# A vision tower on one core: head values in four quarters of the array, and a third pair turned early

## The chip, the cores and the metric

The kernel runs on one NeuronCore of one Trainium2 chip. The metric is the device time of one execution in microseconds (us). A core has five engines that run side by side and wait for each other by semaphores: TensorE (PE in the profile; its weight loads are PEld), VectorE (DVE), ScalarE (ACT), GpSimd (POOL) and SyncE (SP), which here issues most of the DMA transfers. Matrix products are written to PSUM, which has 8 banks of 128 partitions by 512 float32 numbers; everything else lies in SBUF, 128 partitions wide. All data is float32.

## The reference, cut to what matters

The input holds 32 images of 3 x 256 x 256. A tokenizer makes 256 tokens of 256 features of each. Layer 0 is a gated attention and a feed-forward part on selected tokens; layer 1 is a phasor memory and an FFN that is a small attention network of its own, with 4 heads of 64 features and 4 experts. The two parts that the change touches:

```python
def _L0_attn_ref(x, g, W_uv, ...):
    xn = x / jnp.maximum(norm, EPS) * g                 # x is the layer-normed token
    uv = jax.nn.silu(jnp.einsum('bnd,de->bne', xn, W_uv) + b_uv)
    u, v, base = uv[..., :H], uv[..., H:2*H], uv[..., 2*H:]
    q = base * gamma[0] + beta[0]
    k = base * gamma[1] + beta[1]
    attn = jnp.square(jax.nn.relu(einsum('bns,bms->bnm', q, k) * S**-0.5))
    return jnp.einsum('bnh,hd->bnd', u * jnp.einsum('bnm,bmh->bnh', attn, v), W_o) + b_o

def _L1_ffn_ref(x, hl_w, hl_b, wq, wk, wv, gate_w, ...):
    sx = jnp.einsum('bsh,ndh->bnsd', x, hl_w) + hl_b    # 4 heads of 64
    v = jnp.einsum('bnsd,nod->bnso', sx, wv)            # the head values
    ...                                                 # 4 experts: scores, softmax, att @ v
    ...                                                 # gate over the experts, two small layers
```

## The kernel before

The 32 images stay in SBUF as `H[b]` through all layers (two chunks of 128 tokens by 256 features). The work goes in stages: tokenizer (0 to about 180 us), attention of layer 0 (to 690), its feed-forward part (to 915), the memory of layer 1 (to 1246), the FFN of layer 1 (to the end). Within each stage the order of every engine's instructions is the order in which the program emits them (the schedule is by hand), so an instruction that waits holds back all that are emitted after it on its engine. DMA transfers go through SP's queue in the same way.

**Tokenizer and layer-0 attention.** The tokenizer loop (L384) makes one image per step: 12 products into one PSUM bank, emptied by DVE, which also takes the statistics; the patches of an image are loaded by SP five images ahead. Layer 0's attention works on pairs of images. A pair is prepared by `norm_b` (L261: four DVE instructions that normalise into `cx` tiles), `bias_b` (L268: POOL adds the output bias to `H`), and then its activations must be turned, feature-major, into a tile `xT`. There are two ways for that. `turn_b` (L273) transposes on TensorE and copies out of PSUM by ACT and DVE. `blocks_b` (L277) and `turned_b` (L289) do it without TensorE: DVE transposes blocks of 32 x 32 into the tile `blocks` (one buffer), SP stores it by four DMAs to a DRAM tile `b_turned`, and four more DMAs load it back, turned, as `bxT` (two buffers, L293).

Pairs 0 and 1 are normalised inside the tokenizer loop, after images B-6 and B-4, and turned on TensorE: pair 0 before the last image, pair 1 at the start of the attention loop. That loop (L535) is a pipeline by pairs: step t computes scores (`scores_b`), gates and values of pair t-1 (named old), base and queries of pair t (new), the gated product and output of pair t-2 (older), and prepares pair t+1 (next_one). In step t=1 the pair prepared is pair 2, whose `norm_b` and `blocks_b` stand after the gates and whose `turned_b` stands after `bias_b`. `base_b` (L295) of pair 2, in step t=2, is the first to read its `bxT`, directly behind the scores of pair 1.

**FFN of layer 1.** Each image passes through some 97 pieces (`PIECES`). A table `ROUND`, written out by hand, says in which order the pieces of eight images at different depths follow each other in one round; a table `END` does it for the last six images. In a round, TensorE's pieces come in this order: `experts` 0, `scores` 1, 0, 2, `experts` 1, `head_values`, `first_layer`, `heads`, `scores` 5, 4, 3, `second_layer`, and eight `outputs`. All heads have 64 features, and two heads share one 128-row tile, so products of heads have 64 rows. `experts` (L1180), `scores` and `head_values` (L1193) use two row groups of the array, 64 rows each by 128 columns, and write to two banks. `outputs` and `second_layer` use two column halves, 128 rows by 64 columns each. `first_layer` (L1433) and `heads` use the whole array, 128 rows by 128 columns.

`head_values` multiplies `sx` (features of two heads by 128 tokens, the stationary operand) by `WV` (64 rows by 80 columns, the moving operand) for two chunks of tokens, two head pairs and two row groups: 8 products. Each float32 product is two pairs of instructions, a weight load (LDWEIGHTS) and a MATMUL. Both banks of `im.pv` are emptied by DVE in `head_values_out` (L1204). All products are recorded under the helper's line, L118, so in the profile they are told apart by the names of their operands: `WV,sx` are the head values, `sx,A` the experts before them, `fxT,w_fc` the first layer behind them.

Of the kernel before, what the change touches and what calls it, by code (L numbers as in the profile page):

```python
# [40 lines left out]
P = 128  # L41
B, N, D = 32, 256, 256
# [38 lines left out]
def vit_tower(tc, a, out):  # L81
# [35 lines left out]
    def mm(o, lhsT, rhs, first=True, last=True):  # L117
        nc.tensor.matmul(o, lhsT, rhs, start=first, stop=last)  # L118
# [142 lines left out]
    def norm_b(b0, s):  # L261
        s.xs = []
        for j in range(2):
            x = px.tile([P, NC, D], F32, name="cx", bufs=8)
            normed(x, b0 + j, st_b)
            s.xs.append(x)

    def bias_b(b0, s):  # L268
        for j in range(2):
            h = H[b0 + j]  # L270
            nc.gpsimd.tensor_tensor(h, h, over(row_b("b_o"), [P, NC, D], 1), ALU.add)

    def turn_b(b0, s, pool, name):  # L273
        s.xT = pool.tile([P, 2, 2 * N], F32, name=name)
        transposed(s.xT, s.xs, copy_split)

    def blocks_b(b0, s):  # L277
        s.d = pdram.tile([32, 16 * NC, 4, 32], F32, name="b_turned", bufs=2)
        y = px.tile([P, 4 * N], F32, name="blocks", bufs=1)
        y = y.rearrange("p (f c t) -> p f c t", f=8, t=32)  # L280
        for j, x in enumerate(s.xs):
            nc.vector.transpose(
                y[:, :, j * NC : (j + 1) * NC, :].rearrange("p f c t -> p c f t"),
                x.rearrange("p c (f t) -> p c f t", t=32),
            )
        for i in range(4):
            nc.sync.dma_start(s.d[:, :, i, :], y[32 * i : 32 * i + 32].rearrange("p f c t -> p (f c) t"))
# [18 lines left out]
    with (  # L306
        tc.tile_pool(name="a_w", bufs=1) as pw,
        tc.tile_pool(name="a_x", bufs=6) as pp,
    ):


        PARTS = (1, 1, 2, 2)
        x0, tokW = [], []
        for k, n in enumerate(PARTS):
            f = sum(PARTS[:k])
            x, w = pw.tile([P, n, N], F32, name=f"patch0_{k}"), pw.tile([P, n, D], F32, name=f"tokW{k}")
            nc.sync.dma_start(x, patches[:, f : f + n, 0:N])
            nc.scalar.dma_start(w, a["tokW"][:, f : f + n, :])
            x0 += [x[:, i, :] for i in range(n)]
            tokW += [w[:, i, :] for i in range(n)]  # L320
        p = bank()
        for _ in range(3):
            mm(p[:, 0:N], zero[:, 0:P], zero)
        n_k, xs_a = len(tokW), {}

        def load_patches(b):
            xs_a[b] = pp.tile([P, n_k, N], F32, name="patch")
            nc.sync.dma_start(xs_a[b], patches[:, :, b * N : (b + 1) * N])

        load_patches(1)  # L330
        load_patches(2)
        row_a = load_rows(pw, "rows_a", ROWS_A, N_ROWS_A, nc.sync)
        nc.sync.dma_start(cols, a["cols"])
        for b in range(3, 6):
            load_patches(b)

        def layer_0_weights():
            return (
                load(wpool_b, "wuv", nc.sync), load_rows(wpool_b, "rows_b", ROWS_B, N_ROWS_B, nc.sync),
                load(wpool_b, "wo", nc.sync), load_rows(wpool, "rows_c", ROWS_C, N_ROWS_C, nc.sync),  # L340
                load(wpool, "before", nc.sync), load(p0, "w1", nc.sync),
            )

        def unit_a(b):
            if b == 0:
                ps = [bank() for _ in range(NC)]
                for k in range(n_k):
                    for c in range(NC):
                        mm(ps[c][:, 0:D], x0[k][:, c * P : (c + 1) * P], tokW[k], k == 0, k == n_k - 1)
                for c in range(NC):  # L350
                    nc.vector.tensor_tensor(H[b][:, c, :], ps[c][:, 0:D], row_a("tok_b"), ALU.add)
            else:
                x, p = xs_a.pop(b), bank()
                for c in range(NC):
                    for k in range(n_k):
                        mm(p[:, c * D : (c + 1) * D], x[:, k, c * P : (c + 1) * P], tokW[k], k == 0, k == n_k - 1)
                nc.vector.tensor_tensor(
                    H[b], p.rearrange("p (c d) -> p c d", c=NC), over(row_a("tok_b"), [P, NC, D], 1), ALU.add
                )
                if b + 5 < B:  # L360
                    load_patches(b + 5)
            st, _, i = at(st_b, b)
            for c in range(NC):
                stats(st, i, c, H[b][:, c, :])

        def powers_b(b):
            st, rs, i = at(st_b, b)
            q = slice(i * NC, (i + 2) * NC)  # L370
            var = st.rearrange("p i c s -> p (i c) s")[:, q, 1]
            low = spool.tile([P, 2 * NC], F32, name="low")
            pow_rstd(low, var)
            nc.gpsimd.tensor_scalar(rs[:, q], var, 1e-36, 1.0, ALU.max, ALU.mult)
            nc.gpsimd.tensor_tensor(rs[:, q], rs[:, q], minus_half[:, 0 : 2 * NC], ALU.pow)
            return rs[:, q], low

        def factors_b(rs, low):
            nc.vector.scalar_tensor_tensor(rs, low, 1e5, rs, ALU.mult, ALU.min)
            nc.vector.tensor_scalar(rs, rs, col("attn_g"), None, ALU.mult)  # L380

        for b in range(B):  # L384
            if b == B - 1:
                half = [p0.tile([P, 4, D], F32, name="cs", bufs=2).rearrange("p j d -> p (j d)") for _ in range(2)]
                turn_b(0, pairs_b[0], p0, "xsel")
                base_b(0, pairs_b[0], half[0][:, 0 : 2 * N])
                queries_b(0, pairs_b[0], half[0][:, 2 * N :], half[1][:, 0 : 2 * N])
            unit_a(b)  # L390
            if b == 4:
                wuv, row_b, wo, row_c, before, w1 = layer_0_weights()
            if b % 2:
                powers = powers_b(b - 1)
            elif b:
                factors_b(*powers)
            if b in (B - 6, B - 4):
                u = (b - B + 6) // 2
                norm_b(2 * u, pairs_b[u])
                bias_b(2 * u, pairs_b[u])  # L400

    def norm_c(b):
# [35 lines left out]
    with (  # L438
# [96 lines left out]
        for t in range(B // 2 + 2):  # L535
            new, old, older, next_one = pair(t) if t else None, pair(t - 1), pair(t - 2), pair(t + 1)
            next_one = next_one if t else None
            if t == 1:
                turn_b(*new, p2, "bxT")
            if t >= 4:  # L540
                turned = turn_weights(2 * (t - 4))
            if old:
                scores_b(*old)
            if new:
                base_b(*new, p2.tile([P, 2 * N], F32, name="base"))
            if t >= 4:
                ranks(2 * (t - 4), turned)
                if t in (5, 7):
                    first_ranks(2 * t - 10, quads[t // 2 - 2], 0)
            if new:  # L550
                queries_b(*new, p2.tile([P, 2 * N], F32, name="bq"), p2.tile([P, 2 * N], F32, name="bk"))
            if old:
                gates_b(*old)
            if t == 1:
                factors_b(*powers)
            if next_one:
                norm_b(*next_one)
                blocks_b(*next_one)
            if old and t >= 3:
                norms_c(2 * (t - 3))  # L560
            if old:
                values_b(*old)
            if next_one:
                bias_b(*next_one)
            if old and t >= 3:
                residuals_c(2 * (t - 3))
            if next_one:
                turned_b(*next_one, p2, "bxT")
            if t == B // 2 - 1:
                blocks_c(0, quads[0], 0)  # L570
                moved_c(0, quads[0], 0)
            if older:
                gated_b(*older)
                if t == B // 2 + 1:
                    norms_c(2 * (t - 3))
                    residuals_c(2 * (t - 3))
                output_b(*older)
# [531 lines left out]
    with (  # L1109
# [83 lines left out]
        def head_values(b, im):  # L1193
            im.pv = [bank(), bank()]
            for c in range(NC):
                for hp in range(2):
                    o = (2 * c + hp) * VC
                    for s, p in zip(halves, im.pv):
                        mm(p[:, o : o + VC], im.sx[s, hp, c * P : (c + 1) * P], WV[s, hp, :])

        def head_values_out(b, im, h):
            im.v = whole(im, "ev", [P, NC, NH, VC], p2)
# [789 lines left out]
```

## Time and profile before

| | |
|---|---|
| median of 3 runs | 1856.04 us (1854.69 to 1856.21) |
| the profiled execution | 1860.63 us, of it 1858.9 from the first to the last instruction |
| mean granted TensorE clock | 0.989 |
| PE busy in 180 to 690 us (attention, layer 0) | 507.47 us of 510 |
| PE busy in 1246 to 1780 us (FFN, layer 1) | 530.51 us of 534; DVE 470.69, ACT 441.91 |
| last 79 us | PE 50.81, DVE 73.46 |
| head values, `WV,sx` | 512 loads of 188 ns, 512 products of 267 ns mean |

How to read such lines. A timeline row gives the start, the length, the engine, the source line, the operation, the tiles written and read (`out<-in`), for a product rows*columns of the array and then rows x columns of the moving operand, and the count of instructions merged; in brackets stands the idle time before it and what ended it. Matmul durations include the way through the array, so a train of products is better read from the distance of their starts. A row of a table by stretches gives the stretch, its length, the busy time and number of instructions of each engine, the granted clock, the share of the DMA engines and GB/s.

### The profile page before, as it was taken

Reading aid. Unit: us, or ns where it says so; the run is one execution under the profiler, and the core shown is the slowest. Engines: PE = TensorE matmul, PEld = TensorE weight load, DVE = VectorE, ACT = ScalarE, POOL = GpSimd, SP = SyncE. Lnnn points to the kernel's source line nnn. Section 1 sums busy time; section 2 is a strip of 40 time slices with the busy share of each in tenths; the row PEclk is TensorE's granted clock in tenths of the full one; section 3 lists DMA queues with packets and bytes.
Section 4 is the critical chain, followed back from the end, with each engine's and each line's share of the span. In section 5 each row is a group of like instructions: output and inputs, shape, how many; then the busy total and the mean of one; then the engine's idle time right before and its main releaser. Section 6 shows DMA issues by size and latency. Waiting matters only on the chain.

```text
span 1858.9 us, 36581 instructions
## 1 busy us (share of the span) xinstructions
PE 1814.4 (98%) x14284; PEld 1277.1 (69%) x14284; DVE 1345.4 (72%) x3595; ACT 810.0 (44%) x1640; POOL 614.0 (33%) x697
## 2 busy tenths in 40 slices
PE   9999999999999999999999999999999999999993
PEld 7887567676666677676654555557777778778772
DVE  2335477878888664543578778764899999999998
ACT  0001222222222211212244544547888888888883
POOL 1223133434343334333434333323222232222330
PEclk9999999999999999999999999999999999999996
DMA  8551212121212134333321221222344443434432
GB/s 291 165 153 35 46 42 61 52 63 44 59 41 63 37 109 145 108 100 99 96 80 68 91 78 70 80 63 58 101 107 103 106 106 104 108 99 110 101 99 67
DMA packets 193171, 167.50 MB, mean 90 GB/s; under 512 B 70880, under 2 KB 166112, under 8 KB 192608
## 3 DMA queue, kind: packets, MB, share of 16 engines
q1 hardware_dynamic: 186272, 147.51, 28.0%
q0 software_dynamic: 6144, 16.79, 3.1%
q8 instruction: 115, 1.88, 0.4%
q10 hardware_dynamic: 576, 0.79, 0.1%
q14 instruction: 64, 0.52, 0.1%
HBM read 82.98 MB, written 57.41 MB: 76 GB/s over the span
## 4 chain that ended last, share of the span: by engine, by line
PE 92%; DVE 5%; ACT 1%; DMA 1%; issue 1%; SPq 0%; DVEq 0%; ACTq 0%
PE bank L118 91%; DMA patch<-in_patches_dram 0%; PE bank L516 0%; DVE eo L1353 0%; DVE fout L1504 0%; DVE ranges L1376 0%; DVE six L126 0%; ACT dex L945 0%; DVE two L1361 0%; ACT et L1229 0%; ACT two L945 0%; DVE dz L991 0%; DVE dxB L199 0%; DVE dx L837 0%; DMA b_turned<-blocks 0%
## 5 line engine op out<-in xcount | busy, mean ns | idle before, releaser
L1238 POOL TENSOR_SCALAR_AFFINE_SELECT et<-et 128x512 f32<-128x512 f32 (+1 forms) x192 | 170.1, 895 | 395.8 <-ACT et L1229 291.5
L1229 ACT ACTIVATE et<-bank 128x512 f32<-128x512 f32 x384 | 202.7, 625 | 0.1
L118 PE MATMUL bank<-ev,et 128*64 128x72 f32 (+1 forms) x6144 | 194.0, 225 | 2.5 <-ACT et L1229 1.3
L118 PEld LDWEIGHTS bank<-ev,et 128*64 128x64 f32 x6144 | 190.0, 137 | 7.5 <-issue 3.8
L118 PE MATMUL bank<-g,sw 64*128 64x256 f32 (+1 forms) x512 | 178.7, 490 | 0.0
L118 PE MATMUL bank<-g,sx 64*128 64x256 f32 (+1 forms) x512 | 178.3, 489 | 0.0
L118 PE MATMUL bank<-tokW,patch 128*128 128x256 f32 x768 | 169.3, 384 | 2.1 <-DMA patch<-in_patches_dram 2.1
L118 PEld LDWEIGHTS bank<-tokW,patch 128*128 128x128 f32 x768 | 148.0, 193 | 23.7 <-issue 2.9
L118 PE MATMUL bank<-bxT,w_wuv 128*128 128x512 f32 x300 | 132.9, 598 | 2.5 <-DMA bxT<-b_turned 2.5
L118 PEld LDWEIGHTS bank<-g,sx 64*128 64x128 f32 x512 | 92.7, 187 | 52.3 <-issue 43.6
L864 ACT ACTIVATE hT<-bank,cols 128x512 f32<-128x512 f32 x64 | 44.0, 687 | 186.9 <-PE bank L118 186.9
L118 PE MATMUL bank<-wvo,dm 128*128 128x512 f32 x256 | 114.3, 599 | 0.0
L118 PE MATMUL bank<-w_wo,gT 128*128 128x256 f32 x512 | 113.2, 379 | 0.0
L118 PE MATMUL bank<-attn,bv 128*128 128x256 f32 x512 | 113.1, 379 | 0.0
L118 PE MATMUL bank<-w_w,hT 128*128 128x256 f32 x512 | 112.3, 380 | 0.0
L118 PE MATMUL bank<-xsel,w_w 128*128 128x512 f32 x256 | 111.4, 593 | 0.0
L118 PEld LDWEIGHTS bank<-attn,bv 128*128 128x128 f32 x512 | 97.3, 190 | 19.5 <-issue 7.2
L126 DVE BATCH_NORM_STATS2 six<-h 128x6 f32<-128x256 f32 x256 | 105.6, 413 | 4.4
L118 PEld LDWEIGHTS bank<-w_w,hT 128*128 128x128 f32 x512 | 97.1, 190 | 15.5 <-issue 2.9
L118 PEld LDWEIGHTS bank<-w_wo,gT 128*128 128x128 f32 x512 | 97.3, 190 | 13.3 <-DVE gT L489 0.2
L118 PE MATMUL bank<-w_wuv,bxT 128*128 128x512 f32 x240 | 105.5, 592 | 0.0
L118 PEld LDWEIGHTS bank<-bxT,w_wuv 128*128 128x128 f32 x300 | 57.6, 192 | 68.6 <-issue 67.8
(292 smaller groups left out, 3567.9 us busy)
## 6 DMA issues: line engine op xcount, KB each, us to landing
patch<-in_patches_dram SPq DMA_DIRECT2D x31, 768.0 KB, 4.6
exT<-normed SPq DMA_DIRECT2D x32, 256.0 KB, 3.6
sw<-sx SPq DMA_DIRECT2D x64, 128.0 KB, 2.4
er_turned<-eblk SPq DMA_DIRECT2D x31, 256.0 KB, 2.8
fraw<-er_turned SPq DMA_DIRECT2D x62, 128.0 KB, 3.3
both<-fxT SPq DMA_DIRECT2D x62, 128.0 KB, 2.3
both<-hx SPq DMA_DIRECT2D x62, 128.0 KB, 2.3
out_dram<-fout SPq DMA_DIRECT2D x31, 256.0 KB, 2.2
```

The lines of the kernel that those rows point to most:

```text
L118: nc.tensor.matmul(o, lhsT, rhs, start=first, stop=last)
L126: nc.vector.bn_stats(six, x)
L864: nc.scalar.activation(s.hT[:, m, :], p, AF.Gelu_apprx_tanh, bias=col("b1", m))
L1229: nc.scalar.activation(t2[:, i, :], p, AF.Exp)
L1238: nc.gpsimd.affine_select(out=own, in_=own, pattern=[[0, 2 * n_e], [1, P]], compare_op=ALU.is_ge, fill=0.0, base=0, channel_multiplier=-1,)
```

## The change

Two independent edits. In the attention of layer 0, three pairs instead of two are prepared in the tokenizer: after images B-8, B-6 and B-4 pairs 0, 1 and 2 are normalised and get their bias; for pair 2 the block transposes and the four stores to DRAM follow there too. The four loads of pair 2's `bxT` move to the top of step t=1, directly behind pair 1's `turn_b`, and step t=1 prepares no pair any more.

In the FFN of layer 1, each head-value product of 64 rows by 128 columns is made as two of 64 rows by 64 columns: the 128 tokens of a chunk are taken in two halves `q`, and the result of each half goes to the partitions `q` of the same bank. With two row groups, the four products of a step lie in the four quarters of the array. The moving operand, the sums and the banks stay as they are.

```diff
@@ tokenizer loop
-            if b in (B - 6, B - 4):
-                u = (b - B + 6) // 2
+            if b in (B - 8, B - 6, B - 4):
+                u = (b - B + 8) // 2
                 norm_b(2 * u, pairs_b[u])
+                if u == 2:
+                    blocks_b(2 * u, pairs_b[u])
                 bias_b(2 * u, pairs_b[u])
@@ attention loop
             if t == 1:
                 turn_b(*new, p2, "bxT")
+                turned_b(*next_one, p2, "bxT")
...
-            if next_one:
+            if next_one and t > 1:
                 norm_b(*next_one)
                 blocks_b(*next_one)
...
-            if next_one:
+            if next_one and t > 1:
                 bias_b(*next_one)
...
-            if next_one:
+            if next_one and t > 1:
                 turned_b(*next_one, p2, "bxT")
@@ head_values
-                    for s, p in zip(halves, im.pv):
-                        mm(p[:, o : o + VC], im.sx[s, hp, c * P : (c + 1) * P], WV[s, hp, :])
+                    for q in halves:
+                        for s, p in zip(halves, im.pv):
+                            mm(p[q, o : o + VC], im.sx[s, hp, c * P + q.start : c * P + q.stop], WV[s, hp, :])
```

## The prediction

> **What bounds the kernel now.** I read the page first: busy time by engine, the slices and the chain that ended last. TensorE is busy 98% of the span and carries 92% of the chain, and nothing in the page says that another engine sets the time before the last slices. So the change is worth what it takes off TensorE's own stream, or out of a wait in it.
>
> ```profile
> PE 1814.4 (98%) x14284; PEld 1277.1 (69%) x14284; DVE 1345.4 (72%) x3595; ACT 810.0 (44%) x1640; POOL 614.0 (33%) x697
> PE 92%; DVE 5%; ACT 1%; DMA 1%; issue 1%; SPq 0%; DVEq 0%; ACTq 0%
> ```
>
> Second, for the attention edit, the timeline of TensorE where layer 0's attention begins, and the busy time by stretch there (columns: stretch; length; busy PE, PEld, DVE, ACT, POOL; granted clock; DMA):
>
> ```profile
> 197.05 1.89 PE L118 MATMUL bank<-bq,bk 128*128 128x256 f32 x8
> 201.47 10.31 PE L118 MATMUL bank<-bxT,w_wuv 128*128 128x512 f32 x20 [2.53 <-DMA bxT<-b_turned]
> ...
> 198.80:201.40 2.60, 0.14 (x1) 0.00 (x0) 0.00 (x0) 0.83 (x2) 2.04 (x2) 0.94 0.39 130
> 201.40:204.80 3.40, 3.33 (x5) 1.56 (x6) 0.00 (x0) 0.00 (x0) 0.00 (x0) 0.55 0.02 5
> 204.80:215.00 10.20, 10.20 (x25) 4.52 (x24) 5.15 (x9) 4.06 (x6) 2.64 (x2) 1.00 0.32 50
> ```
>
> See two things: TensorE stands still for 2.5 us until the third pair's transposed activations land, and then it gets 0.55 of its clock for 3.4 us. The chain of waits there says why they land so late (DVE normalises, turns blocks, SP issues four stores, then four loads):
>
> ```profile
> 186.69 2.24 DVE cx L177 x4
> 188.93 1.22 DVE blocks L282 x2
> ...
> 192.34 3.39 DMA b_turned<-blocks
> ...
> 198.29 3.05 DMA bxT<-b_turned
> ```
>
> Third, for the FFN edit, one steady round in TensorE's timeline, and the groups by shape (mean ns of one after the busy time):
>
> ```profile
> 1417.06 1.03 PE L118 MATMUL bank<-sx,A 64*128 64x256 f32 x8
> 1417.92 1.02 PE L118 MATMUL bank<-WV,sx 64*128 64x80 f32 x16
> 1418.87 1.12 PE L118 MATMUL bank<-fxT,w_fc 128*128 128x512 f32 x2
> 1419.83 1.89 PE L118 MATMUL bank<-exT,w_hl_t 128*128 128x256 f32 x8
> ...
> L118 PEld LDWEIGHTS bank<-WV,sx 64*128 64x128 f32 x512 | 34.9, 188 | 1.7 <-ACT et L1229 0.2 <-issue 0.2
> L118 PEld LDWEIGHTS bank<-ev,et 128*64 128x64 f32 x6144 | 190.0, 137 | 7.5 <-issue 3.8 <-ACT et L1229 2.1 <-DVE eo L1353 0.8
> L118 PE MATMUL bank<-W,both 128*64 128x68 f32 x992 | 37.7, 229 | 4.3 <-DMA both<-hx 3.0 <-DVE fgate L1477 1.1
> ...
> 1400.00:1500.00 100.00, 100.00 (x1672) 79.39 (x1670) 94.02 (x257) 84.38 (x204) 31.04 (x35) 1.00 0.43 107
> ```
>
> The block of 16 head-value instructions owns TensorE for 0.95 us of each round. In this stage TensorE is never idle and rounds repeat every 17.86 us; DVE is busy 94%, ACT 84%.
>
> **What the skill says.** The Trainium skill, "TensorE: Matmul & The Clock Gate", section "LDWEIGHTS (loading the stationary operand)": a load's time goes with its columns, not its rows, columns/1.2 in ns. The trace agrees: a 128-column load is 51 ns longer than a 64-column one (188 against 137), so a load occupies 53 ns per 64 columns. The same page, "The mechanism": loads overlap running products only where the row groups differ. The trace differs: the 64-column products of the attention outputs (`ev,et`, all 128 rows, two column halves) run 192 instructions in 5.94 us, 31 ns each, though each load needs 53; so column halves do overlap, and the measurement decides. "TensorEngine Tiling (Array Packing)", "Key Properties": changing the tiling mode drains the array, and tiles run independently. The trace agrees on the drain: about 92 ns from the end of one mode's stream to the next mode's first load (scores to `W,both`), and then the first load is exposed (`W,both` first product 274 ns instead of 223, so 51). Four quarters at once, two of them on the same rows, no run here shows. The clock page's Part 1, "What's actually happening", has half clock for a window of about 3.4 us after an idle one: the stretch at 0.55 above agrees.
>
> **The change, part 1: third pair turned in the tokenizer.** Removed from step t=1: four normalisations (2.33 us DVE), two block transposes (1.29), two bias additions (2.7 on POOL), four stores and four loads issued at the end of that chain. Added: one more normalisation and bias group at b=24, and two transposes and four stores at b=28; the four loads move to the top of t=1.
> Cover: in the tokenizer DVE does about 1.9 us per image plus at most 2.7 at even ones, against 5.16 us of TensorE; at b=28 it becomes about 5.9, so image 29's bank is emptied some 0.55 us later. One bank of eight is taken per image, so TensorE doesn't notice, and DVE idles 3.3 us before image 30. POOL has 11.7 us free in that stretch. On SP the last patch load is issued at b=26, so nothing stands behind the four stores until t=1's loads; those four (2.5 us of issue and 3.05 us to landing) start when the last patches are used up, at about 179.5, and land by about 185, 14 us before their reader at 198.8. Without that cover, every microsecond late comes back as wait.
> Gain: the score products' stream ends at 198.77; products run at full rate again from 204.75, and only four of them lie between, which cost 4 x 0.427 = 1.71 at full clock. 204.75 - 198.77 - 1.71 = 4.27 us, of which 2.7 is idle and about 1.55 the half clock. Next in line at t=2 are the fourth pair's loads, whose distance from t=3 doesn't change, so nothing takes the wait's place. I take -4.25 us; bounds -3.5 (half-clock window falling elsewhere) to -4.4.
>
> **Part 2: four quarters.** Before: a product is two load/matmul instructions. Two row groups run side by side (starts 6 to 7 ns apart), and the pairs follow each other at 112 ns. Streaming 80 columns takes 67 ns (512 columns of the same type take 427), the 128-column load 107: the block is bound by loads. From the first start at 1417.92 to the end of its last stream at 1418.78 it is 853 ns, and it enters free of cost, because the products before it (`sx,A`) have the same mode: the first follows 209 ns after the last of those, whose stream is 213.
> After: 32 instruction pairs with 64-column loads (53 + 5 ns), so the stream of 80 columns becomes the bound: 67 + 3 (the 68- and 72-column rows lose 2.4 to 3 per slot) = 70 ns per slot of four instructions, one in each quarter, 8 slots = 557, and some 20 for the staggered start. New in front: the mode changes from 64*128 to 64*64, 92 + 51 = 143. The change behind the block, to 128*128, exists already. 143 + 577 = 720, against 853: 133 ns less per image. 512 matmuls and 512 loads are added in all.
> Who is late next: `hx` on ACT starts 38 ns after the first-layer product ends in nearly every round, 16 ns after the preceding exponent; in the round at 1527.26, where it didn't wait, it began 144 ns before that ended, so ACT can follow by about 160 ns. The scores behind need ACT's copy of `g`, done at 1421.68, at 1422.62, so 0.9 us are in hand. DVE has about 1 us per round. The wait that is added, the drain, holds back the first layer alone, and that begins earlier all the same.
> Counted are 29 images; the first rounds (TensorE waits for ACT at 1266) and the last image, beside a DVE-bound end, give nothing. 29 x 0.133 = 3.9 us. Bounds per image: -276 ns (no drain) to +405 (below).
>
> Sum: -4.25 - 3.85 = -8.1 us. The profiled execution took 1860.63 (span 1858.9 and 1.7 around it), 4.6 above the median of the three runs; the differences are absolute, so I take them from 1856.04: 1847.9.
>
> **Rivals.**
> - Slower: the two column halves of one row group take turns. Then each row group streams 16 instructions in a line, 16 x 70 = 1115, with the entry 1258 ns: +405 per image, x 29 = +11.7, and with -4.25 the time is 1863.5. It decides once the block exceeds 853 + 274 = 1127 ns. For it: the skill's sentence on row groups, and no four-quarter run here. Against it: `ev,et`.
> - Instruction supply: 64 instructions in a slot train of 9 ns each; the densest long stretch before is 14.7 ns (`W,both`, 64 in 945 ns). At 14.7 the block is 941 + 143 = 1084: +231, +6.7 in all, 1858.5. Bursts of four within 9 ns speak against a limit there. Somewhere between is likelier, about 1855.
> - The FFN gain is hidden by ACT or DVE: only part 1 counts, 1851.8. For it: 84% and 94% busy; against: the margins above.
> - No drain between 64*128 and 64*64: 29 x 0.276 = 8.0, 1843.8.
> - The attention edit doesn't do what it says (the loads still land late, or DVE's extra work stalls the tokenizer): about 1852.2.
>
> **Numbers.** Chances: forecast 0.60, turns 0.07, supply 0.10, hidden 0.12, no drain 0.08, attention edit void 0.03. Range 1843 to 1855: it takes in no drain, hidden, and half of supply. Beyond 0.2% (3.7 us), what a measurement of this kernel tells from no change: faster 0.60 + 0.08 + over half of hidden + a little of the rest = 0.78; same, from hidden, supply and void, 0.13; slower, from turns and the worst of supply, 0.09. Alone, the forecast runs from 1846 to 1850.
>
> **What would show it.** Part 1: no wait for `bxT` near 198.8, the clock there 1.00, and `bxT` products straight after the scores. Part 2: 64*64 head-value groups with twice the count and loads near 135 ns; 0.35 us instead of 0.21 from the last `sx,A` to the first head-value product; the block about 0.58 us; rounds of 17.73 instead of 17.86. I'm wrong if rounds lengthen (turns or supply), if a wait for ACT stands in front of the scores (hidden), or if the half clock appears at another place in the attention.

## The result and the profile after

| | before | after |
|---|---|---|
| median of 5 runs each, on one chip | 1856.04 us (1854.69 to 1857.08) | 1848.07 us (1846.83 to 1849.88) |
| ratio after to before | | 0.9957, 95% interval 0.9947 to 0.9968 |

That is 8.0 us less (5.9 to 9.8 by the interval); forecast were 8.1.

The head of the page of the kernel after:

```profile
span 1845.0 us, 37605 instructions
...
PE 1805.2 (98%) x14796; PEld 1259.7 (68%) x14796; DVE 1339.8 (73%) x3595; ACT 807.5 (44%) x1640; POOL 617.2 (33%) x697
...
PE 91%; DVE 6%; ACT 1%; DMA 1%; issue 0%; SPq 0%; ACTq 0%; DVEq 0%
```

TensorE still carries the end. The two spans differ by 13.9 us, more than the medians do, so the pair of traces can't be subtracted as a whole. It has to be taken apart by stage, at marks that both kernels have, and each part asked whether it comes back in other executions:

| distance between marks on TensorE, us | before | after | difference |
|---|---|---|---|
| start to the first `bxT` product (tokenizer) | 181.60 | 179.31 | -2.29 |
| from there to the first product of layer 1's memory (attention and FFN of layer 0) | 733.56 | 729.30 | -4.26 |
| from there to the first `heads` product (memory of layer 1) | 328.43 | 326.62 | -1.81 |
| start of the first to start of the last block of `heads` products (FFN of layer 1) | 534.53 | 528.98 | -5.55 |
| from there to the last `W_last,both` product (second layer of the last image) | 66.05 | 66.06 | 0 |

The first row depends on when the first transfers arrive, and on the clock there: over all 13 traces of this document it is 181.1 to 181.7 where TensorE got half its clock for 3.4 us at about 9 us, and 177.6 to 180.3 where it did not, and both kinds occur with the attention edit and without. The third row is 326.6 in one_more_switch and 328.4 in cols_first and layer_in_quarters, which are the same as the kernel after up to the end of that stage. Those 4.1 us are chance. The second and fourth rows are the change, though the fourth has some 1.3 us of chance in it, as will be seen.

**Attention.** The timeline of TensorE after, from the score products on, and the windows of the same stretch (us, then busy time and count for PE, PEld, DVE, ACT, POOL; clock; DMA share; GB/s):

```profile
194.76 1.89 PE L118 MATMUL bank<-bq,bk 128*128 128x256 f32 x8
196.49 8.75 PE L118 MATMUL bank<-bxT,w_wuv 128*128 128x512 f32 x20
```

```profile
190.00:198.80 8.80, 8.80 (x26) 4.72 (x25) 2.58 (x4) 3.94 (x7) 1.92 (x2) 1.00 0.01 2
198.80:201.40 2.60, 2.60 (x7) 1.17 (x7) 2.27 (x6) 0.98 (x2) 0.66 (x2) 1.00 0.00 0
```

The bracket with its 2.53 us of waiting for `b_turned` is gone, the `bxT` products follow the scores at once, and the clock is 1.00.

**FFN.** One round of TensorE's timeline after, then its groups by shape (busy time and mean ns of one, then idle time before):

```profile
1424.63 1.03 PE L118 MATMUL bank<-sx,A 64*128 64x256 f32 x8
1425.59 0.78 PE L118 MATMUL bank<-WV,sx 64*64 64x80 f32 x32
1426.30 1.12 PE L118 MATMUL bank<-fxT,w_fc 128*128 128x512 f32 x2
1427.26 1.89 PE L118 MATMUL bank<-exT,w_hl_t 128*128 128x256 f32 x8
```

```profile
L118 PEld LDWEIGHTS bank<-WV,sx 64*64 64x64 f32 x1024 | 19.9, 132 | 11.0 <-ACT et L1233 9.7 <-issue 1.0 <-ACT fxT L1420 0.3
...
L118 PE MATMUL bank<-WV,sx 64*64 64x80 f32 x1024 | 25.1, 235 | 0.0
```

```profile
1400.00:1500.00 100.00, 100.00 (x1760) 77.63 (x1754) 94.95 (x277) 84.33 (x205) 29.96 (x34) 1.00 0.40 103
```

TensorE is busy throughout, as before. The block of head values runs 0.78 us instead of 1.02, with its trail (the way through the array), but begins 0.96 us after `sx,A` began instead of 0.86. That is the drain of the added change of tiling mode, from 64*128 to 64*64, with a first load that nothing covers. Single records say the rest. The starts of the 32 products, in ns from the first, and of the 16 before:

```
after:  0 7 14 20 | 120 127 134 140 | 190 196 203 210 | 259 265 272 279 | ... | 535 542 549 555
before: 0 6 | 70 76 | 181 188 | 293 300 | 405 411 | 516 523 | 628 635 | 740 746
```

Four quarters start within 20 ns. The second four come 120 ns after the first, of which 51 are that load; from then on there are four every 69 ns, near the stream of 67. Before, two started together, and from the second pair on the next two came 111 to 112 ns later. From the end of the last `sx,A` stream to the end of the last head-value stream it is 715 ns. The median round is 17.723 us instead of 17.859.

### The profile page after: what moved, and what is told of

The parts are those of the page before. It is cut to its first block, busy times and chain, and to the rows that moved or that the text cites. A ratio compares the mean times of both kernels' runs of the same rounds, so it can differ in the third digit from the quotient of the medians.

```text
span 1845.0 us, 37605 instructions
## 1 busy us (share of the span) xinstructions
PE 1805.2 (98%) x14796; PEld 1259.7 (68%) x14796; DVE 1339.8 (73%) x3595; ACT 807.5 (44%) x1640; POOL 617.2 (33%) x697
## 3 DMA queue, kind: packets, MB, share of 16 engines
q8 instruction: 119, 1.95, 0.5%
## 4 chain that ended last, share of the span: by engine, by line
PE 91%; DVE 6%; ACT 1%; DMA 1%; issue 0%; SPq 0%; ACTq 0%; DVEq 0%
PE bank L118 90%; DVE eo L1357 1%; PE bank L518 0%; DVE six L126 0%; DMA patch<-in_patches_dram 0%; DVE ranges L1380 0%; DVE fout L1508 0%; DVE dx L840 0%; DVE two L1365 0%; DVE dxB L199 0%; ACT et L1233 0%; DMA er_turned<-eblk 0%; DMA fraw<-er_turned 0%; ACT two L948 0%; DVE dz L994 0%
## 5 line engine op out<-in xcount | busy, mean ns | idle before, releaser
L118 PEld LDWEIGHTS bank<-w_w,hT 128*128 128x128 f32 x512 | 97.0, 190 | 15.6 <-issue 2.9
L1262 ACT COPY eo<-bank 128x280 f32<-128x280 f32 x256 | 91.6, 401 | 22.4 <-PE bank L118 19.6
```

Of the source, the lines that this page charges most:

```text
L1262: nc.scalar.copy(im.o[:, g * OC : (g + 1) * OC], p[:, 0:OC])
```

## The experiments

Ratios are to the kernel before on the same chip, with their 95% interval. All kernels compute the whole reference.

### Each half of the change by itself

attn_only is the kernel after with the old products of `head_values`; quarters_only is the kernel before with the new ones:

```diff
-                    for s, p in zip(halves, im.pv):
-                        mm(p[:, o : o + VC], im.sx[s, hp, c * P : (c + 1) * P], WV[s, hp, :])
+                    for q in halves:
+                        for s, p in zip(halves, im.pv):
+                            mm(p[q, o : o + VC], im.sx[s, hp, c * P + q.start : c * P + q.stop], WV[s, hp, :])
```

> The kernel before with the attention edit alone. Theory (idle plus half clock removed, nothing takes their place): 4.3 us faster than before, about 1851.8, with the FFN rounds still at 17.86 us. Rival (the edits help each other, or the gain is only the 2.5 us of the wait): 2.5 us or less. Rival (the FFN edit makes the whole gain): no difference.

> The kernel before with the FFN edit alone. Theory (loads of 64 columns hide under the stream, one drain added): 137 ns less in each of about 29 rounds, 4.0 us faster, about 1852.1, and the half clock near 201 us still there. Rival (ACT or DVE set the round, and the shorter rounds of the changed kernel are fewer stalls in instruction issue): within 1.5 us of before.

| | median, us | ratio | worked out | attention and FFN of layer 0 | median round |
|---|---|---|---|---|---|
| attn_only | 1853.62 | 0.9983 (0.9976 to 0.9990) | -3.2 us (-4.5 to -1.9) | 729.30 | 17.859 |
| quarters_only | 1851.90 | 0.9973 (0.9964 to 0.9982) | -5.0 us (-6.7 to -3.3) | 733.71 | 17.722 |

Each edit works alone, in its own stage, and the sum of the two, -8.2, is the whole, -8.0, well within the intervals. In quarters_only the old wait and the half clock stand where they stood; its timeline and a window of it:

```profile
199.46 4.76 PE L118 MATMUL bank<-bxT,w_wuv 128*128 128x512 f32 x7 [2.65 <-DMA bxT<-b_turned]
```

```profile
199.40:202.80 3.40, 3.34 (x5) 1.55 (x6) 0.00 (x0) 0.00 (x0) 0.00 (x0) 0.54 0.02 5
```

### Does the third pair have to be turned in the tokenizer?

top_of_step is the kernel before, with the third pair's preparation, all but its bias, moved only to the top of step t=1, behind `turn_b` of pair 1:

```diff
             if t == 1:
                 turn_b(*new, p2, "bxT")
+                norm_b(*next_one)
+                blocks_b(*next_one)
+                turned_b(*next_one, p2, "bxT")
...
-            if next_one:
+            if next_one and t > 1:
                 norm_b(*next_one)
                 blocks_b(*next_one)
...
-            if next_one:
+            if next_one and t > 1:
                 turned_b(*next_one, p2, "bxT")
```

> The kernel before, with pair 2's normalisation, block transposes, stores and loads moved to the top of step t=1, directly behind pair 1's turning, and nothing of it in the tokenizer; its bias stays where it was. DVE begins this chain at about 181.7 us instead of 186.7, so the loads should land at about 196.4, 2 us ahead of their reader. Theory (only the landing time counts): 4.3 us faster than before, as with the tokenizer. Rival (DVE's chain in front of the query copies and the loads beside them hold back something else, or 5 us are not enough): less than 2 us faster.

1853.43 us, ratio 0.9983 (0.9977 to 0.9990), attention and FFN of layer 0 729.30: the same as attn_only to the last digit. SP's queue and TensorE in its timeline:

```profile
183.72 3.09 SPq L287 DMA_DIRECT2D b_turned<-blocks  x4
...
189.85 2.51 SPq L293 DMA_DIRECT2D bxT<-b_turned  x4
...
198.25 6.17 PE L118 MATMUL bank<-bxT,w_wuv 128*128 128x512 f32 x14
```

The last load's issue ends at 192.36, 5.9 us ahead of the reader, and no bracket stands before the `bxT` products. So only the landing counts. In the kernel after, the last load lands at 180.94, 15.6 us ahead of its reader at 196.49: more than is needed.

half_early moves only the first of the two images' normalisation to the top of t=1 (one run; `norm_b` gets the images it shall do as an argument):

```diff
...
             if t == 1:
                 turn_b(*new, p2, "bxT")
+                norm_b(*next_one, (0,))
...
-                norm_b(*next_one)
+                norm_b(*next_one, (1,) if t == 1 else (0, 1))
```

> The kernel before with only the first image of pair 2 normalised at the top of step t=1: DVE's chain before the loads gets 1.2 us shorter, so the loads should land 1.2 us earlier and TensorE waits about 1.4 us instead of 2.6. Theory (the half clock follows only where most of a window of 3.4 us was idle): the clock stays 1.00, and from the first product of the attention to the first of layer 1's memory the time is 2.7 us shorter than before (730.8 against 733.56), more than the wait saved. Rival (any wait of a microsecond brings the half clock): 1.2 us shorter.

1856.18 us. The wait fell by 0.5 us only, to 2.07, no half clock followed, and the stage took 731.61, 1.95 less than before, more than the wait saved. It was to show whether a shorter wait escapes the half clock. The next kernel shows that a wait of full length can escape it too, so the length alone doesn't decide; what does is read there from both.

### Is the block bound by its loads, and do the quarters overlap?

narrow_before doubles loads and products of the kernel before and leaves the streamed work equal, by cutting the moving operand into two halves of 40 columns:

```diff
-                    for s, p in zip(halves, im.pv):
-                        mm(p[:, o : o + VC], im.sx[s, hp, c * P : (c + 1) * P], WV[s, hp, :])
+                    for x in (0, VC // 2):
+                        for s, p in zip(halves, im.pv):
+                            mm(p[:, o + x : o + x + VC // 2], im.sx[s, hp, c * P : (c + 1) * P], WV[s, hp, x : x + VC // 2])
```

> The kernel before with the moving operand of each head-value product cut into two of 40 columns: the columns streamed stay the same, the loads of 128 columns double. Theory (the block before is bound by its loads, 112 ns each): the block doubles, 0.89 us more per image, 26 us slower than before, about 1882. Rival (the block was bound by the stream or by something else that goes with the columns): within 3 us of before.

1883.9 us, ratio 1.0142 (1.0124 to 1.0160), some 26 us more; rounds of 18.719. The block takes 1598 ns between its first and last start instead of 746. Pairs follow each other at 105 to 112 ns as before, though they stream half as much: loads bound the old block, and the stream was hidden under them.

In the attention, which this edit doesn't touch, something else was to be seen. Its timeline and two windows:

```profile
201.45 2.81 PE L118 MATMUL bank<-bxT,w_wuv 128*128 128x512 f32 x6 [2.63 <-DMA bxT<-b_turned]
```

```profile
198.80:201.40 2.60, 0.02 (x1) 0.00 (x0) 0.00 (x0) 0.71 (x2) 2.03 (x2) 1.00 0.39 129
201.40:204.80 3.40, 3.35 (x8) 1.63 (x9) 0.64 (x2) 0.69 (x1) 0.00 (x0) 1.00 0.02 5
```

The same wait, 2.63 us, and no half clock behind it: 8 products in the 3.4 us where the kernel before and quarters_only had 5. The stage took 732.17, against 733.56 and 733.71.

The traces say why. In all 13 of them every stretch at one granted clock, except the last, which the end cuts off, is a whole multiple of 3.413 us long, so the clock changes only at marks 3.413 us apart; and these marks lie differently in each execution. Windows between marks, first of the kernel before, then of narrow_before:

```profile
197.65:201.06 3.41, 1.29 (x6) 0.78 (x5) 0.29 (x1) 1.66 (x3) 1.89 (x2) 1.00 0.46 154
201.06:204.48 3.42, 3.01 (x4) 1.49 (x5) 0.00 (x0) 0.00 (x0) 0.14 (x1) 0.50 0.02 5
...
197.27:200.68 3.41, 1.55 (x8) 1.02 (x6) 0.55 (x1) 1.66 (x3) 1.63 (x2) 1.00 0.47 153
200.68:204.09 3.41, 2.64 (x6) 1.25 (x7) 0.00 (x0) 0.65 (x1) 0.40 (x1) 1.00 0.02 5
```

| | wait, us | of it in the window where it began | in the next | half clock in the next |
|---|---|---|---|---|
| before | 2.53 | 2.12 | 0.41 | yes |
| quarters_only | 2.65 | 2.29 | 0.36 | yes |
| narrow_before | 2.63 | 1.86 | 0.77 | no |
| half_early | 2.07 | 1.42 | 0.65 | no |

Up to 1780 us, the 13 traces have seven windows in which TensorE was idle for 2.06 us or more (2.06 to 2.41), and a window at half clock followed each; it followed none of the others, which were idle for 1.86 us at most. So the idle time within one window decides, and it is chance where the marks cut a wait.

rows_apart (from the kernel after) makes all products of one row group before those of the other, so that at first only the two column halves of the same rows can overlap; cols_first only exchanges the two inner loops:

```diff
 rows_apart
-            for c in range(NC):
-                for hp in range(2):
-                    o = (2 * c + hp) * VC
-                    for q in halves:
-                        for s, p in zip(halves, im.pv):
+            for s, p in zip(halves, im.pv):
+                for c in range(NC):
+                    for hp in range(2):
+                        o = (2 * c + hp) * VC
+                        for q in halves:
 cols_first
-                    for q in halves:
-                        for s, p in zip(halves, im.pv):
+                    for s, p in zip(halves, im.pv):
+                        for q in halves:
```

> The changed kernel with all eight products of row group 0 ahead of all eight of row group 1, so that only the column halves of one row group can run side by side. Theory (TensorE passes over only some three products that wait, so distant ones can't fill a free quarter): 16 slots of 70 ns instead of 8, about 0.5 us per image, 15 us slower than the changed kernel, about 1863. Rival (a free quarter fetches its next product from anywhere in the queue): no slower.

> The changed kernel with the two loops exchanged: the two column halves of a row group follow each other, then the other row group. Theory (each quarter takes its next product as soon as it is free, within a few instructions' reach): the same slots of 69 ns, the same time within 1 us. Rival (the order in the program decides which quarters run side by side, and column halves of the same rows don't): up to 0.5 us per image more, 15 us.

rows_apart: 1859.77 us, ratio 1.0015 (1.0008 to 1.0022); rounds of 18.049, 326 ns more than after. cols_first: 1847.98, ratio 0.9951 (0.9932 to 0.9970); rounds of 17.723 and the starts of the kernel after. Starts of rows_apart in ns:

```
0 7 | 120 127 | 190 196 | 259 265 | 328 335 | 340 347 | 397 404 | 460 466 467 473 |
530 535 536 542 | 599 605 | 668 675 | 737 744 | 806 813 | 875 882
```

Inside one row group the column halves start 6 to 7 ns apart and the next two 69 ns later: they overlap. The gain goes because half of the array stands idle. Not quite half: at 340 ns the other row group begins, though six MATMUL instructions (three float32 products) of the first, which stand ahead of it in the kernel, are still to start, two each at about 397, 466 and 535. That saves some three slots, the difference between the 882 ns seen and 16 times 69.

### What does a change of mode cost?

one_more_switch is the kernel after with `first_layer` put ahead of `head_values` in the table, so that the mode changes once more; layer_in_quarters makes `first_layer`, whose matrix is block-diagonal, as two 64*64 quarters behind the head values, which takes away its own change of mode and leaves one ahead of `heads`, as many as after:

```diff
 one_more_switch, in ROUND
-            (-6, 7), (-6, 9), (-2, 69), (-4, 50), ...
+            (-6, 7), (-2, 69), (-6, 9), (-4, 50), ...
 layer_in_quarters
+            if b <= B - 6:
+                for q in halves:
+                    mm(im.ph[q], fc1[q, q], im.fT[q].rearrange("p k n -> p (k n)"))
+                return
```

> The changed kernel with the first layer's product put between the experts and the head values, instead of behind the head values. The array then goes 64*128, 128*128, 64*64, 128*128 where it went 64*128, 64*64, 128*128: one switch more, with its drain (92 ns) and an exposed load of 128 columns (107). Theory (switches cost TensorE time, and rounds are as long as TensorE's stream): 0.2 us more per round, 5.8 us slower than the changed kernel, about 1854. Rival (a drain is hidden, or ACT, which gets the first layer's product 0.7 us earlier, sets the round): no slower than the changed kernel.

> The changed kernel with the first layer's product alone as two of 64*64 on the diagonal quarters, in its old place. The switch behind the head values moves behind the first layer, so there are as many; the stream of two quarters side by side is as long as the one of the whole array. Theory (only the number of switches counts): rounds within 20 ns of 17.72, the same time within 1 us. Rival (quarters cost something of their own, or the two row groups can't write one bank at a time, as here): the product takes up to twice its 0.85 us, 25 us slower.

one_more_switch: 1857.19 us, ratio 0.9999 (0.9990 to 1.0007), rounds of 17.920: 197 ns for one change. By the medians that takes back what both edits gained. In its trace the FFN is 5.3 us longer than after (534.28), as the price of one change asks, and the end of the program, which wasn't counted in, 1.3 (67.33); the rest of the difference between the medians isn't explained by it. layer_in_quarters: 1850.57, ratio 0.9967 (0.9955 to 0.9979), rounds of 17.723 exactly, so the number of changes decides and not which products stand between them. The intervals of this kernel and the one after overlap.

### Can a change of mode be taken out?

fewer_switches makes `first_layer` as above and `heads` as 128*64 column halves placed behind the scores, directly ahead of the second layer's 128*64 products, with the experts' second part earlier; four changes of mode in a round instead of five. fewer_switches_2 puts exponents and masking of two scores back to where they were:

```diff
 fewer_switches, heads
-                    mm(p[:, hp * N : (hp + 1) * N], hl[:, k, hp * P : (hp + 1) * P], im.f[:, k], k == 0, k == 1)
+                    for q in halves:
+                        o = hp * P
+                        mm(p[q, hp * N : (hp + 1) * N], hl[:, k, o + q.start : o + q.stop], im.f[:, k], k == 0, k == 1)
 fewer_switches_2, in the new order of the round
-            (-5, 24), (-1, 91), ... (-2, 70), (-5, 20), (-5, 26), (-3, 64), ...
+            (-5, 20), (-5, 24), (-5, 26), (-1, 91), ... (-2, 70), (-3, 64), ...
```

> The changed kernel with one mode switch less per round: the first layer's product as two of 64*64 on the diagonal quarters (its weights are block-diagonal), so that it shares the head values' mode; the heads as two column halves of 64, placed behind the scores and in front of the second layer, which is in column halves already; the experts' second product and ACT's copies of it two places earlier, so that the scores behind them find g ready. Theory (rounds are TensorE's stream, and each switch costs a drain of 92 ns and an exposed load): 0.2 us less in each of some 30 rounds, 6 us, about 1842. Rival (the order was balanced against ACT and DVE, which are busy 84 and 94 of 100, and TensorE now waits for them): as slow as the changed kernel or slower.

> fewer_switches with ACT's exponents of scores part 2, and POOL's masking of them, put back in front of ACT's squares and of hx. In fewer_switches DVE's gating of the expert outputs took 2.14 us and the scaling behind it 1.57, where they take 1.22 and 0.69 otherwise, just while POOL masked the exponents of parts 2 and 5. Theory (DVE is slowed by POOL working beside it, and DVE became the bound): the gating falls back to 1.2 us, since POOL is done a microsecond earlier; the scaling stays slow, as the masking of part 5 stays; rounds shorten from 18.82 to about 18.0 us, 1856 in all or a little less, still slower than the changed kernel. Rival (DVE waits for ACT or for its banks, and the long instructions only show that): gating stays at 2.1 us and the rounds at 18.8.

Both lost: 1878.98 us, ratio 1.0120 (1.0104 to 1.0135), rounds of 18.822; and 1875.43, ratio 1.0103 (1.0086 to 1.0120), rounds of 18.710. DVE's groups by shape in the kernel after, and in fewer_switches, over the same 450 us of the FFN:

```profile
L1357 DVE TENSOR_TENSOR eo<-eo,gate 128x1024 f32<-128x1024 f32 x52 | 63.5, 1221 | 0.9
L1392 DVE TENSOR_TENSOR er<-er,hv 128x512 f32<-128x512 f32 x26 | 17.8, 684 | 0.0
```

```profile
L1364 DVE TENSOR_TENSOR eo<-eo,gate 128x1024 f32<-128x1024 f32 x48 | 79.5, 1656 | 0.8
L1399 DVE TENSOR_TENSOR er<-er,hv 128x512 f32<-128x512 f32 x24 | 37.7, 1570 | 0.0
```

The same instructions take 1656 ns instead of 1221 and 1570 instead of 684. Two and one of them in a round make 2 x 0.435 + 0.886 = 1.76 us, where DVE had 5% of 17.72, 0.9 us, to spare; the rest, 0.86, is most of the 1.10 us by which the round grew. The timeline of fewer_switches shows what lies beside them, POOL's masking of the scores:

```profile
1437.59 2.14 DVE L1364 TENSOR_TENSOR eo<-eo,gate 128x1024 f32<-128x1024 f32 x1
1439.65 1.57 DVE L1399 TENSOR_TENSOR er<-er,hv 128x512 f32<-128x512 f32 x1
```

```profile
1437.56 1.09 POOL L1249 TENSOR_SCALAR_AFFINE_SELECT et<-et 128x1024 f32<-128x1024 f32 x1 [1.93 <-ACT et L1240]
1439.02 1.66 POOL L1249 TENSOR_SCALAR_AFFINE_SELECT et<-et 128x1024 f32<-128x1024 f32 x1 [0.37 <-ACT et L1240]
```

In the kernel after, the maskings start at 1427.54 and 1432.22, just before and just after DVE's three (1428.93 to 1431.9). The Trainium skill, "SBUF — State Buffer", section "Who interferes with whom", says it: a VectorE instruction with two SBUF inputs contends with a GpSimd instruction that reads SBUF, and the later one is held up until the first is done. The gating that began 0.03 us behind a masking of 1.09 lasted 0.92 longer than its mean in the kernel after, which agrees. fewer_switches_2 is the test: with a masking moved away from the gating, that is back at 1218, while the scaling, still beside one, stays at 1575:

```profile
L1364 DVE TENSOR_TENSOR eo<-eo,gate 128x1024 f32<-128x1024 f32 x48 | 58.5, 1218 | 0.8
L1399 DVE TENSOR_TENSOR er<-er,hv 128x512 f32<-128x512 f32 x24 | 37.8, 1575 | 0.0
```

But the round stayed 0.99 us above the kernel after's, and 0.89 of DVE would just have fitted into the slack. TensorE's starts show where the time goes. In each of 18 rounds in the middle of the stage, the 16 score products behind the first layer take 3.11 us from the first start to the last, instead of 2.26 in the kernel after: 0.85 of the 0.99. In each of these rounds one of them, on one of the two banks, starts 0.05 us after the end of DVE's first `ev` (L1215), which empties a bank of head values; and that stands on DVE behind a reduction that waits for ACT, where the exponents now go ahead of `esq`:

```profile
1435.32 0.69 DVE L1387 TENSOR_REDUCE ranges<-esq 128x8 f32<-128x512 f32 x1 [0.72 <-ACT esq L1383]
1435.92 0.48 DVE L1215 TENSOR_TENSOR ev<-bank,ones_row 128x320 f32<-128x320 f32 x1
```

In fewer_switches the score products take 3.16 us and wait for the same `ev`, but there DVE doesn't wait for ACT. This is read from the traces; no run took that wait out. No kernel tried beats the one after by more than its interval.

## Why the prediction came out right

The mechanism was right for both edits. That the sum came out within 0.2 us is in part luck: two sizes were off, in opposite directions.

- **"bounds -3.5 (half-clock window falling elsewhere) to -4.4", taken -4.25: the size was off.** 4.27 was made of "2.7 is idle and about 1.55 the half clock". The idle part always goes. The half clock was in two of the three profiled executions with a wait of 2.5 to 2.65 us, and absent in narrow_before. So the edit is worth 729.30 against 732.17, 2.9 us, where it is absent, and 4.3 to 4.4 where it isn't. The ratio of attn_only says 3.2 (1.9 to 4.5), and that of top_of_step the same. The term should have been the idle part with a share of 1.55, and the bound -2.7. An estimate of the share: if a half clock takes about 2 us of idle time in one window of 3.41, a wait of 2.6 falls so in some 0.6 of all placements of the marks, and the edit is worth 2.9 + 0.6 x 1.4, about 3.7, on average. One profile was taken for every execution.
- **"the fourth pair's loads, whose distance from t=3 doesn't change, so nothing takes the wait's place": right.** The stage fell by the whole amount and no new bracket came.
- **Cover in the tokenizer, that DVE and SP carry the added work: right as far as seen.** Of the traces without a half clock in the tokenizer, attn_only, with the added work, has 179.5 to the first `bxT` product, and quarters_only, without it, 179.5; of those with one, layer_in_quarters has 181.4 with the work, and the kernel before 181.6 without it. The loads were issued from 176.0 us and landed by 180.9 instead of 179.5 and 185, which changes nothing in the sum.
- **"8 slots = 557, and some 20 for the staggered start", "92 + 51 = 143": right to a few ns.** 69 instead of 70 per slot; 93 from the last `sx,A` stream to the first new load, and 51 of that load exposed; 715 for 720.
- **"133 ns less per image", "Counted are 29 images": the size was off.** It is 137, in 31 rounds: the first four rounds shortened too, from 51.29 to 50.75, four times 0.135; the last image gave nothing, as said. 31 x 0.137 = 4.25 instead of 3.9. quarters_only measured 5.0 (3.3 to 6.7), and 4.25 lies within. The pair of traces has more, 5.55, because single rounds are longer by chance, by 1.9 us in all before and 0.3 after; attn_only, without the edit, had 1.0.
- **"ACT can follow by about 160 ns": right, and just enough.** `hx` still begins 38 ns after the first layer's product ends. It used to begin 16 ns after the recorded end of the instruction ahead of it on ACT, and now begins 126 ns before that end, so 142 ns of the 160 are used. No wait for ACT stands ahead of the scores.

The rivals: "turns" falls by the starts of the four quarters within 20 ns; instruction supply, by 64 instructions in some 560 ns, under 9 ns each; "hidden", by the rounds, which fell by all of 137; "no drain", by the 93 ns and by one_more_switch; "void", by attn_only. Where the gain in the FFN comes from can now be put in one sentence: the streamed work is the same, eight times 67 to 70 ns, but a load of 64 columns fits under it and one of 128, at 112 ns between pairs, did not.

## What to carry to other kernels

Set the load of a product beside its stream: where the load is longer (here 107 ns beside 67), halving the stationary columns into two column groups makes the stream the bound, but an added change of tiling mode costs about 0.14 to 0.2 us and has to be paid out of it. A transfer needs to land just before its reader, and how much earlier is worth nothing; price its wait by the bare idle time and put a clock penalty behind it in as a chance, not a certainty; here it came when some 2 us of a wait fell into one window. Before an order is changed for TensorE's sake, look at which two-input DVE instructions it puts beside POOL's.

## What the runs showed of the hardware

- Waits of 2.53 and 2.65 us brought a half clock for 3.4 us, and one of 2.63 did not; 2.06 us of idle time within one window of 3.413 were enough, and 1.86 were not. The Trainium skill, "TensorE: Matmul & The Clock Gate", Part 1, "What's actually happening", has the activity window free-running and 3413 ns long, and the marks in the traces agree. It gives one idle window of about 3.4 us for the fall to half clock; here less than a whole one was enough, and the measurement decides.
- TensorE started MATMUL instructions of one row group ahead of up to six waiting ones of the other that stand before them in the program (rows_apart). Within that reach the order in which the quarters are written made no difference (cols_first).
- Two DVE instructions with both inputs in SBUF stretched from 1.22 to 2.14 us and from 0.68 to 1.57 beside POOL's masking.
